# A two-layer graph network on one core: moving the Elu sums and two weight preparations to other places in the queues

## Chip, core and metric

The kernel runs on one core of one Trainium2 chip. The metric is the device time of one execution in microseconds; the time before is the median of three executions, 3022.03 us (3021.59 to 3023.15). The core has five engines with a queue of instructions each: TensorE (PE in the profile, its weight loads PEld), VectorE (DVE), ScalarE (ACT), GpSimd (POOL), and SyncE (SP), which here issues the transfers. Each queue runs in order; across queues, instructions wait for each other by semaphores.

## What is computed

64 graphs of 256 nodes with 512 features share one adjacency matrix `adj`. Two layers follow each other, both with a normalisation in front and a residual around them. The reference, cut to what matters:

```python
# layer 0: masked attention, 8 heads of 64
h = relu(layernorm(x))
q, k, v = h @ Wq + bq, h @ Wk + bk, h @ Wv + bv          # split into heads
scores = q @ k^T / 8 + (1 - adj) * -1e9
x = x + (softmax(scores) @ v) @ Wo + bo
# layer 1: graph attention
h = relu(layernorm(x)) @ W
e = leaky_relu(h @ a1 [rows] + h @ a2 [columns], 0.2) * adj
x = x + elu(softmax(e) @ h + beta * h)
```

All of it is float32.

## The kernel before

Every product with a weight is done in seven block products in place of eight (a 2 x 2 scheme with sums of blocks of the activations and differences of blocks of the weights). So each weight matrix is kept as seven blocks: four are loaded, and `combine` makes four differences of them once at the start, one of which takes the place of a loaded block. Each block product ends in a *tap*, which copies or adds its PSUM bank to its place.

```python
def products(aT, sums, wt, columns, name, taps, across=False):
    plan = (("u", ..., B11), ("v", sums[:, 0], T1), ("u", sums[:, 1], T2), ("c", ..., B21),
            ("u", sums[:, 2], T3), ("v", sums[:, 3], B22), ("u", ..., T4N))
    for (bank, lhs, w_i), tap in zip(plan, taps):      # three banks of ps_mm: u, v, c
        ...                                            # matmuls into the bank
        done = tap(ps)
        if done is not None:
            LAST["tap"] = done                         # the last tap that ran on VectorE and returned itself
        yield                                          # the caller runs so many products at a time
```

For q/k (`project_qk`, line 238) the taps of products 1, 3, 4, 5, 6 and 7 are VectorE additions (lines 311 and 320: q0, k0, q0, k1, k0, q1) and that of product 2 is four ScalarE instructions (line 316). For v and for the second layer's h (lines 330 and 334) products 1, 2, 3 and 7 are copied by ScalarE and 4, 5 and 6 are added by VectorE. For the attention's output `po` all are VectorE additions (line 403). PSUM is shared out in two pools: `ps_big` (2 buffers) and `ps_mm` (4 buffers: q/k, v, output and h products, the transposes `tr_h` and `tr_g`, the two `av`, and a few smaller ones).

The sums and stores of the last step, of graph b:

```python
def gat_sum(b):                      # after the second layer's attention
    ...
    m = p2.tile([P, D], F32, tag="t", ...)      # exp of the row, ScalarE
    o = p2.tile([P, D], F32, tag="o", ...)      # relu of the row, ScalarE
    G[b].append((m, o))

def gat_store(b, t, after=None):     # t: one half of the nodes
    m, o = G[b][t]
    with behind(after):              # queued on its engine after that instruction, no wait for it
        nc.vector.scalar_tensor_tensor(o, m, 1.0, o, op0=ALU.min, op1=ALU.add)                    # L465
        nc.vector.scalar_tensor_tensor(o, o, -1.0, X[b][:, t, :], op0=ALU.add, op1=ALU.add)       # L466
    nc.sync.dma_start(out[b, t * P:(t + 1) * P, :], o)
```

The preparations of the weights Wo and W (Wo with the bias of v worked in):

```python
def prepare_o():
    ps = ps_mm.tile([P, D], F32, tag="mm", name="bvwo")
    nc.vector.tensor_copy(bvb, bv_sb...)                  # bv, each element over a row
    ...                                                   # 16 matmuls: ps = bv @ Wo
    nc.vector.tensor_tensor(bo_sb, bo_sb, ps, ALU.add)    # L186
    nc.scalar.mul(wo_sb[:, :4], wo_sb[:, :4], 1.0 / O_SCALE)
    combine(wo_sb, nc.gpsimd)                             # 4 differences

def prepare_h():
    for j in range(2):
        aj = ...                                          # a1 or a2 on all partitions, by a transfer
        for half in range(2):
            for c in range(2):
                nc.vector.scalar_tensor_tensor(prod, w_sb[...], 1.0 / E_SCALE, aj, ...)     # L199
                nc.vector.tensor_reduce(w_sb[..., FH:FE], prod..., ALU.add)                 # L201
    combine(w_sb, nc.vector)                              # 4 differences
```

And the loop over graphs. TensorE's queue follows the program's order; the order of the other queues is made by the compiler's scheduler from priorities (earlier in the program is higher) and its own timing. One pass works on four graphs at once: b in layer 0, b + 1 in its q/k and v, b - 1 in layer 1, b - 2 in the last sums.

```python
    combine(wqk_sb, nc.vector)
    for b in range(min(2, B)):
        norm(b); norm_apply(b); norm_t(b)
        if b == 0:
            run(project_qk(0), 8)
            prepare_v()
            run(project_v(0), 8)
    prepare_adj()
    for b in range(B + 1):
        ...
        scores(b, (0, 1)); residual(b) if b > 0
        run(project_o(b - 1), 8)
        scores(b, (2, 3), after=LAST.get("pow_y"))
        norm(b + 2)
        qk = project_qk(b + 1)
        run(qk, 1)
        after = LAST["tap"]
        gat_store(b - 2, 0, after)
        gat_norm_apply(b - 1, after)              # shift_y on VectorE, ln_y on ScalarE
        run(qk, 2)
        after = LAST["tap"]
        norm_apply(b + 2, after)                  # shift_x on VectorE, ln_x on ScalarE
        gat_store(b - 2, 1, after)
        load(b + 3)
        run(qk, 2)
        gat_norm_t(b - 1)                         # transposes tr_g, h2T, sums h2sum on VectorE
        run(qk, 3)
        run(gat_h(b - 1), 8)                      # products ph
        values(b)                                 # den, rden, av, oT, osum
        gat_scores(b - 1)
        if b == 0:
            prepare_o(); residual(0); prepare_h()
        norm_t(b + 2)                             # transposes tr_h, hT, hsum
        pv = project_v(b + 1)
        run(pv, 4); gat_sum(b - 1); run(pv, 4)
```

The conditions on b (`if nxt`, `if prev`, `if old`) are left out here. `scores` on GpSimd multiplies each tile of exponentials with the mask (L364) and adds its halves (L366); `residual` adds the bias to x there (L397).

Of the kernel before, what the change touches and what calls it, by code (L numbers as in the profile page):

```python
# [8 lines left out]
F32 = mybir.dt.float32  # L9
AF = mybir.ActivationFunctionType  # L10
ALU = mybir.AluOpType
AX = mybir.AxisListType
PSUM = bass.MemoryType.PSUM

P = 128
# [5 lines left out]
E_SCALE = 2.0 ** -20  # L21
V_SCALE = 2.0 ** -20
D_SCALE = 2.0 ** -60
O_SCALE = 2.0 ** 40
# [4 lines left out]
def tile_gnn_fast(ctx: ExitStack, tc: tile.TileContext, x, adj, wq, bq, wk, bk, wv, bv, wo, bo, w, a, beta, out,  # L29
# [22 lines left out]
    nc = tc.nc  # L52
    B, N, D = x.shape
    H = 8
    HD = D // H
    NT = N // P
    DC = D // P
    NPAIR = H // 2
    HG = H // 4
    HQ = HD // 2  # L60
    FH = D // 2
# [12 lines left out]
    def load(b):  # L74
        X[b] = p2.tile([P, NT, D], F32, tag="x", name=f"x_{b}", bufs=5)
        nc.sync.dma_start(X[b], x[b].rearrange("(t p) c -> p t c", p=P))
# [15 lines left out]
    def combine(wt, eng):  # L92

        for dst, m, n in ((T1, B12, B11), (T3, B22, B12), (T2, B22, T1), (T4N, B21, T2)):
            eng.tensor_tensor(wt[:, dst], wt[:, m], wt[:, n], ALU.subtract)
# [7 lines left out]
    def row(name, src):  # L103
        t = const.tile([P, src.shape[0]], F32, name=name)
        nc.sync.dma_start(t, src.partition_broadcast(P))
        return t
# [10 lines left out]
    for half in range(2):  # L117
        for j in range(2):
            nc.sync.dma_start(wv_sb[:, BLOCKS[half][j]],
                              wv[:, j * FH:(j + 1) * FH].rearrange("(h c p) f -> h p c f", h=2, p=P)[half])  # L120
    if B > 2:
        load(2)


    wo_sb = const.tile([P, 7, 2, FH], F32, name="wo")
# [1 line left out]
    for i in range(4):  # L127
        rows = slice(i * HQ, (i + 1) * HQ)
        for g in range(HG):
            for j in range(2):  # L130
                nc.sync.dma_start(wo_sb[rows, BLOCKS[g][j]],
                                  wo[:, j * FH:(j + 1) * FH].rearrange("(g i d p) f -> i g p d f", g=HG, i=4, d=2)[i, g])
            with nc.allow_non_contiguous_dma(reason="a bias, once"):
                nc.sync.dma_start(bv_sb[rows, g], bv.rearrange("(g i d p) -> i g p d", g=HG, i=4, d=2)[i, g])
    bo_sb = row("bo", bo)

    w_sb = const.tile([P, 7, 2, FE], F32, name="w")
    for half in range(2):
        for j in range(2):
            nc.sync.dma_start(w_sb[:, BLOCKS[half][j], :, :FH],  # L140
                              w[:, j * FH:(j + 1) * FH].rearrange("(h c p) f -> h p c f", h=2, p=P)[half])
    beta_sb = row("beta", beta)

    hs = const.tile([P, NT, 2, FE + 2], F32, name="hs")
    nc.gpsimd.memset(hs[:, :, 1, FE:FE + 1], 1.0)
# [6 lines left out]
    def prepare_adj():  # L152

        some = p3.tile([P, NT], F32, tag="some", name="some", bufs=1)
        empty = p3.tile([P, NT], F32, tag="empty", name="empty", bufs=1)
        full = p2.tile([P, NT, N], F32, tag="g", name="full")
        nc.vector.tensor_reduce(some, adj_sb, AX.X, ALU.add)
        nc.vector.tensor_scalar(empty, some, 0.0, None, ALU.is_equal)
        nc.vector.tensor_scalar(some, some, 0.0, None, ALU.is_gt)
        nc.vector.tensor_reduce(count[:, 1:2], some, AX.X, ALU.add)  # L160
        nc.vector.tensor_tensor(full, adj_sb, adj_sb, ALU.mult)
        nc.vector.tensor_tensor(full, full, adj_sb, ALU.is_equal)
        nc.vector.tensor_reduce(count[:, 0:1], full.rearrange("p t k -> p (t k)"), AX.X, ALU.add)
        for t in range(NT):
            nc.vector.tensor_scalar(full[:, t, :], adj_sb[:, t, :], empty[:, t:t + 1], None, ALU.add)
        ps = ps_mm.tile([P, NT, N], F32, tag="mm", name="adj_t")
        for k in range(NT):
            for t in range(NT):
                nc.tensor.transpose(ps[:, k, t * P:(t + 1) * P], full[:, t, k * P:(k + 1) * P], ident)
        nc.vector.tensor_scalar(adjT, ps, E_SCALE, None, ALU.mult)  # L170
# [4 lines left out]

    def prepare_o():

        ps = ps_mm.tile([P, D], F32, tag="mm", name="bvwo")
        bvb = p2.tile([P, HG, 2, P], F32, tag="t", name="bvb")
        nc.vector.tensor_copy(bvb, bv_sb.unsqueeze(3).to_broadcast([P, HG, 2, P]))  # L180
        for j in range(2):
            for g in range(HG):
                for d in range(2):
                    nc.tensor.matmul(ps[:, j * FH:(j + 1) * FH], bvb[:, g, d, :], wo_sb[:, BLOCKS[g][j], d, :],
                                     start=(g + d == 0), stop=(g + d == 2))
        nc.vector.tensor_tensor(bo_sb, bo_sb, ps, ALU.add)  # L186
        nc.scalar.mul(wo_sb[:, :4], wo_sb[:, :4], 1.0 / O_SCALE)
        combine(wo_sb, nc.gpsimd)

    def prepare_h():  # L190

        for j in range(2):
            aj = p2.tile([P, 2, FH], F32, tag="o", name=f"a_{j}")
            nc.sync.dma_start(aj.rearrange("p i f -> p (i f)"), a[j * D:(j + 1) * D, 0].partition_broadcast(P))
            for half in range(2):
                first, second = BLOCKS[half]
                for c in range(2):
                    prod = p2.tile([P, 2, FH], F32, tag="t", name=f"prod_{j}_{half}_{c}")
                    nc.vector.scalar_tensor_tensor(prod, w_sb[:, first:second + 1:second - first, c, :FH],  # L199
                                                   1.0 / E_SCALE, aj, op0=ALU.mult, op1=ALU.mult)  # L200
                    nc.vector.tensor_reduce(w_sb[:, BLOCKS[half][j], c, FH:FE], prod.rearrange("p i f -> p (i f)"),  # L201
                                            AX.X, ALU.add)
        combine(w_sb, nc.vector)


    def block(aT, t, half):
# [42 lines left out]
    def run(steps, n):  # L249
        for _ in range(n):  # L250
            next(steps, None)

    def behind(ins):

        return tc.issue_after(ins.ins) if ins is not None else nullcontext()
# [83 lines left out]
    def project_v(b):  # L339

        v = V[b] = p2.tile([P, NT, D], F32, tag="v", name=f"v_{b}", bufs=1)
        yield from products(HT[b], HSUM[b], wv_sb, FH, f"pv_{b}",
                            natural_taps(lambda t, j: v[:, t, j * FH:(j + 1) * FH]))
        del HT[b], HSUM[b]
# [117 lines left out]
    def gat_store(b, t, after=None):  # L462
        m, o = G[b][t]
        with behind(after):
# [3 lines that stand above are left out]
        if t == NT - 1:  # L468
            del X[b], G[b]

    with tc.manual_schedule(engines={mybir.EngineType.PE}):
        combine(wqk_sb, nc.vector)
        for b in range(min(2, B)):
            norm(b)
            norm_apply(b)
            norm_t(b)
            if b == 0:
                run(project_qk(0), 8)
                prepare_v()
                run(project_v(0), 8)  # L480
        prepare_adj()

        for b in range(B + 1):
            here, nxt, prev, old = b < B, b + 1 < B, 0 <= b - 1, 0 <= b - 2
            if here:
                scores(b, (0, 1))
                if b > 0:
                    residual(b)
            if prev:
                run(project_o(b - 1), 8)  # L490
            if here:
                scores(b, (2, 3), after=LAST.get("pow_y"))
            if b + 2 < B:
                norm(b + 2)
            qk = project_qk(b + 1) if nxt else iter(())
            run(qk, 1)
            after = LAST["tap"] if nxt else None
            if old:
                gat_store(b - 2, 0, after)
            if prev:  # L500
                gat_norm_apply(b - 1, after)
            run(qk, 2)
            after = LAST["tap"] if nxt else None
            if b + 2 < B:
                norm_apply(b + 2, after)
            if old:
                gat_store(b - 2, 1, after)
            if b + 3 < B:
                load(b + 3)
            run(qk, 2)  # L510
            if prev:
                gat_norm_t(b - 1)
            run(qk, 3)
            if prev:
                run(gat_h(b - 1), 8)
            if here:
                values(b)
            if prev:
                gat_scores(b - 1)
            if b == 0:  # L520
                prepare_o()
                residual(0)
                prepare_h()
            if b + 2 < B:
                norm_t(b + 2)
            pv = project_v(b + 1) if nxt else iter(())
            run(pv, 4)
            if prev:
                gat_sum(b - 1)
            run(pv, 4)  # L530
        for t in range(NT):
            gat_store(B - 1, t)
# [229 lines left out]
```

## Time and profile before

| | before |
|---|---|
| time, median of three | 3022.03 us |
| span of the profiled execution | 3023.4 us |
| granted TensorE clock, mean | 0.993 |
| GpSimd busy | 1867.1 us (62%) |
| ScalarE busy | 1086.8 us (36%) |
| moved from and to memory | 39.85 MB read, 33.55 MB written |

Busy time is the time in which an engine executes, added up; a line of a group gives the busy time, the mean of one instruction and then the idle time of that engine just in front of the group, with what ended it. A line of the waits reads: who waited, for whom, total us, number of times, the longest. A line of the timeline reads: start in us, duration in us, engine, line of the source, operation, output and inputs, shapes, how many were merged; in brackets the idle time in front and what ended it. The span falls into a start of about 125 us, some 61 passes of the loop that are alike, and an end of about 80 us in which no next graph is left.

### The profile page before, as it was taken

The numbers are of one execution on the slowest core, as the hardware profiler recorded it, in microseconds if no ns is written. First come the engines' busy times: TensorE is split into PE (matmuls) and PEld (weight loads), VectorE is DVE, ScalarE is ACT, GpSimd is POOL, SyncE is SP. The second block draws the span as 40 slices with busy tenths as digits, with TensorE's granted clock in tenths as the row PEclk, the third lists the DMA queues.
The fourth block names the chain that finished last, engine by engine and source line by source line (L and its number), as shares of the span: only waits on it lengthen the run. The fifth ranks groups of instructions, "written<-read, shape, count | busy, mean of one in ns | idle before, by whom it ended". The sixth has DMA issues, their size and how long they took to land.

```text
span 3023.4 us, 52940 instructions
## 1 busy us (share of the span) xinstructions
PE 2915.5 (96%) x21910; PEld 2469.9 (82%) x21910; DVE 1907.0 (63%) x3244; ACT 1086.8 (36%) x1987; POOL 1867.1 (62%) x1427
## 2 busy tenths in 40 slices
PE   7999999999999999999999999999999999999996
PEld 6888888888888888888888888888888888888884
DVE  7656656666666566566666665665666666656654
ACT  2333333333333333334333333333343333333332
POOL 6765756656666656566566566575565665666742
PEclk9999999999999999999999999999999999999997
DMA  3000000000000000000000000000000000000000
GB/s 119 15 15 29 22 21 29 18 25 29 15 29 29 15 29 23 21 29 19 25 29 15 29 29 15 29 24 20 29 18 26 29 15 29 29 15 29 22 15 15
DMA packets 43173, 76.86 MB, mean 25 GB/s; under 512 B 5424, under 2 KB 8752, under 8 KB 42928
## 3 DMA queue, kind: packets, MB, share of 16 engines
q1 hardware_dynamic: 42928, 73.42, 7.5%
q8 instruction: 175, 2.87, 0.4%
q14 instruction: 70, 0.57, 0.1%
HBM read 39.85 MB, written 33.55 MB: 24 GB/s over the span
## 4 chain that ended last, share of the span: by engine, by line
PE 86%; DVE 9%; issue 3%; POOL 1%; ACT 0%; DMA 0%; SPq 0%; POOLq 0%; ACTq 0%; DVEq 0%
PE qk_u L238 12%; PE sc L355 8%; PE pg L445 8%; PE po_u L242 8%; PE ph_u L242 7%; PE qk_v L238 7%; PE av L384 7%; PE pv_u L242 7%; DVE o L466 4%; PE ph_v L242 4%; PE po_v L242 4%; PE pv_v L242 4%; PE den L374 2%; PE ph_c L242 2%; PE po_c L242 2%
## 5 line engine op out<-in xcount | busy, mean ns | idle before, releaser
L364 POOL TENSOR_TENSOR s<-s,adjT 128x1024 f32<-128x1024 f32 x256 | 634.6, 2479 | 8.8 <-ACT s L359 7.0
L359 ACT ACTIVATE s<-sc 128x1024 f32<-128x1024 f32 x256 | 248.3, 1021 | 442.2 <-PE sc L355 429.2
L366 POOL TENSOR_TENSOR e<-s 128x512 f32<-128x512 f32 x256 | 351.1, 1371 | 15.3
L427 POOL COPY s1b<-hs 128x256 f32<-128x256 f32 x64 | 25.4, 397 | 522.0 <-ACT hs L330 522.0
L388 POOL TENSOR_TENSOR oT<-oT,rden 128x512 f32<-128x512 f32 x128 | 191.5, 1496 | 241.4 <-PE av L384 222.2
L403 DVE TENSOR_TENSOR x<-po_u,x 128x256 f32<-128x256 f32 x256 | 107.5, 420 | 264.9 <-PE po_u L242 264.9
L377 DVE RECIPROCAL rden<-den 128x512 f32<-128x512 f32 x64 | 214.9, 3357 | 89.4 <-PE den L374 89.4
L238 PE MATMUL qk_u<-hT,wqk 128*128 128x128 f32 x2048 | 258.8, 280 | 2.7 <-DVE kT L320 2.7
L238 PEld LDWEIGHTS qk_u<-hT,wqk 128*128 128x128 f32 x2048 | 241.0, 193 | 24.3 <-issue 20.9
L238 PE MATMUL qk_u<-hsum,wqk 128*128 128x128 f32 x2048 | 251.2, 276 | 5.7 <-DVE kT L311 4.5
L355 PE MATMUL sc<-qT,kT 64*128 64x256 f32 x2048 | 255.8, 389 | 0.3 <-ACT s L359 0.3
L238 PE MATMUL qk_v<-hsum,wqk 128*128 128x128 f32 x2048 | 249.6, 275 | 0.0
L238 PEld LDWEIGHTS qk_u<-hsum,wqk 128*128 128x128 f32 x2048 | 240.2, 193 | 6.3 <-DVE kT L311 4.8
L445 PE MATMUL pg<-hs,eT 128*128 128x256 f32 (+1 forms) x1024 | 238.2, 386 | 7.0 <-ACT eT L436 7.0
L330 ACT COPY hs<-ph_u 128x257 f32<-128x257 f32 x192 | 71.7, 373 | 473.2 <-PE ph_u L242 473.2
L238 PEld LDWEIGHTS qk_v<-hsum,wqk 128*128 128x128 f32 x2048 | 238.9, 192 | 0.0
L355 PEld LDWEIGHTS sc<-qT,kT 64*128 64x128 f32 x2048 | 187.2, 186 | 59.8 <-issue 42.0
L384 PE MATMUL av<-s,v 128*32 128x256 f32 x4096 | 232.7, 379 | 0.0
L445 PEld LDWEIGHTS pg<-hs,eT 128*128 128x128 f32 x1024 | 196.9, 193 | 37.6 <-ACT eT L436 7.8
L216 POOL TENSOR_TENSOR hsum<-hT 128x256 f32<-128x256 f32 x128 | 91.4, 735 | 210.1 <-ACT m L457 197.7
L466 DVE SCALAR_TENSOR_TENSOR o<-o,x 128x512 f32<-128x512 f32 x128 | 212.2, 1658 | 2.1
L384 PEld LDWEIGHTS av<-s,v 128*32 128x32 f32 x4096 | 133.0, 110 | 88.3 <-issue 0.4
(129 smaller groups left out, 5947.9 us busy)
## 6 DMA issues: line engine op xcount, KB each, us to landing
x<-in_x_dram SPq DMA_DIRECT2D x64, 512.0 KB, 3.8
out_dram<-o SPq DMA_DIRECT2D x128, 256.0 KB, 2.1
wqk<-in_L_gnn_Wq_dram SPq DMA_DIRECT2D x2, 512.0 KB, 6.4
wqk<-in_L_gnn_Wk_dram SPq DMA_DIRECT2D x2, 512.0 KB, 7.5
wv<-in_L_gnn_Wv_dram SPq DMA_DIRECT2D x4, 256.0 KB, 5.7
wo<-in_L_gnn_Wo_dram SPq DMA_DIRECT2D x16, 64.0 KB, 2.1
w<-in_L_gnn_W_dram SPq DMA_DIRECT2D x4, 256.0 KB, 5.5
a<-in_L_gnn_a_dram SPq DMA_DIRECT2D x2, 256.0 KB, 6.0
```

The lines of the kernel that those rows point to most:

```text
L238: nc.tensor.matmul(ps[:, d * P:(d + 1) * P], wt[:, w_i, c, d * P:(d + 1) * P], lhs[:, c, :], start=fresh and c + d == 0, stop=(c == 1), sk ...
L242: nc.tensor.matmul(ps, lhs[:, c, :], wt[:, w_i, c, :], start=fresh and c == 0, stop=(c == 1), skip_group_check=True)
L355: nc.tensor.matmul(ps[:, h, t, :], KT[b][hs_, hp, t * P:(t + 1) * P], QT[b][hs_, hp, :], start=True, stop=True)
L359: nc.scalar.activation(s.rearrange("p h k q -> p (h k q)"), ps.rearrange("p h k q -> p (h k q)"), AF.Exp, scale=QSCALE)
L364: nc.gpsimd.tensor_tensor(flat, flat, adjT.rearrange("p k q -> p (k q)").unsqueeze(1) .to_broadcast([P, 2, NT * N]), ALU.mult)
L366: nc.gpsimd.tensor_tensor(e2, s[:, :, 0, :], s[:, :, 1, :], ALU.add)
L377: nc.vector.reciprocal(rden, den)
L384: nc.tensor.matmul(ps[i * HQ:(i + 1) * HQ, d, :], V[b][:, k, c0:c0 + HQ], S[b, 2 * g + i // 2][:, i % 2, k, :], start=(k == 0), stop=(k == ...
L388: nc.gpsimd.tensor_tensor(oT[:, g], oT[:, g], rden[:, g].unsqueeze(1).to_broadcast([P, 2, N]), ALU.mult)
L403: return lambda ps: nc.vector.tensor_tensor(m, ps, m, ALU.add)
L445: nc.tensor.matmul(ps[:, j, :n], eT[:, k, t * P:(t + 1) * P], hs[:, k, j, :n], start=(k == 0), stop=(k == NT - 1))
L466: nc.vector.scalar_tensor_tensor(o, o, -1.0, X[b][:, t, :], op0=ALU.add, op1=ALU.add)
```

## The change

Three things move; hardly any arithmetic changes.

1. Both halves of `gat_store(b - 2)` and the load of graph b + 3 are put behind the seventh product of q/k: the sums are queued on VectorE behind the last tap that reads q/k's banks. Before, one half stood behind the first tap and one behind the third. The aim is that the sums don't stand between TensorE's banks and their readers.
2. `prepare_o` runs right after the first graph's v, before the second graph's transposes, so that its work on ScalarE and GpSimd lies beside the first scores. The scaling of Wo now comes before the product with bv, and the sum scales the product back. In the loads, the bias of v comes after all of Wo, and x of graph 2 after W and beta.
3. `prepare_h` keeps its place in the program, but its VectorE instructions are queued behind the last tap of the second graph's q/k.

```diff
-    if B > 2:
-        load(2)
 ... (loads of Wo: the eight loads of bv move out of their loop, to after it)
     beta_sb = row("beta", beta)
+    if B > 2:
+        load(2)
 ...
     def prepare_o():
+        nc.scalar.mul(wo_sb[:, :4], wo_sb[:, :4], 1.0 / O_SCALE)
         ps = ps_mm.tile([P, D], F32, tag="mm", name="bvwo")
 ...
-        nc.vector.tensor_tensor(bo_sb, bo_sb, ps, ALU.add)
-        nc.scalar.mul(wo_sb[:, :4], wo_sb[:, :4], 1.0 / O_SCALE)
+        nc.vector.scalar_tensor_tensor(bo_sb, ps, O_SCALE, bo_sb, op0=ALU.mult, op1=ALU.add)
         combine(wo_sb, nc.gpsimd)
-    def prepare_h():
+    def prepare_h(after):
+        with behind(after):
 ... (the body as before, indented)
                 run(project_v(0), 8)
+                prepare_o()
 ...
             run(qk, 1)
             after = LAST["tap"] if nxt else None
-            if old:
-                gat_store(b - 2, 0, after)
             if prev:
                 gat_norm_apply(b - 1, after)
             run(qk, 2)
             after = LAST["tap"] if nxt else None
             if b + 2 < B:
                 norm_apply(b + 2, after)
-            if old:
-                gat_store(b - 2, 1, after)
-            if b + 3 < B:
-                load(b + 3)
             run(qk, 2)
             if prev:
                 gat_norm_t(b - 1)
             run(qk, 3)
+            if old:
+                for t in range(NT):
+                    gat_store(b - 2, t, LAST["tap"] if nxt else None)
+            if b + 3 < B:
+                load(b + 3)
 ...
             if b == 0:
-                prepare_o()
                 residual(0)
-                prepare_h()
+                prepare_h(LAST["tap"])
```

## The prediction

> **What bounds the kernel now.** I read the page's first table first: TensorE is busy 96% of the span, VectorE 63%, GpSimd 62%, so TensorE is the engine to fill, and 3023.4 − 2915.5 = 108 us of it are idle. Then I asked the waits (who waited for whom: total us, times, longest) and the groups by line. These lines carry the argument:
>
> ```profile
> PE 2915.5 (96%) x21910; PEld 2469.9 (82%) x21910; DVE 1907.0 (63%) x3244; ACT 1086.8 (36%) x1987; POOL 1867.1 (62%) x1427
> ...
> PE tr_g L283 <- DVE qT L320: 61.2, 61, 1.0
> ...
> L466 DVE SCALAR_TENSOR_TENSOR o<-o,x 128x512 f32<-128x512 f32 x128 | 212.2, 1658 | 2.1
> L465 DVE SCALAR_TENSOR_TENSOR o<-m,o 128x512 f32<-128x512 f32 x128 | 164.1, 1282 | 0.0
> ```
>
> The second line is more than half of TensorE's idle time, and it is one wait: 61 times, once in nearly every graph, 1.0 us each. The two groups below it are the Elu sums. Their means, 1658 and 1282 ns, are far above their shortest forms (678 and 677 ns when I asked for each line by itself), so they are held up by something. The timeline of one graph in the middle shows by what:
>
> ```profile
> 1018.13 0.69 DVE L311 TENSOR_TENSOR kT<-qk_u,bk 128x512 f32<-128x512 f32 x1 [0.29 <-PE qk_u L238]
> 1018.74 0.25 DVE L272 SCALAR_TENSOR_TENSOR shift_x<-mv,rstd_x 128x2 f32<-128x2 f32 x1
> 1018.91 0.68 DVE L465 SCALAR_TENSOR_TENSOR o<-m,o 128x512 f32<-128x512 f32 x1
> 1018.93 2.89 POOL L364 TENSOR_TENSOR s<-s,adjT 128x1024 f32<-128x1024 f32 x1
> ...
> 1019.63 2.74 DVE L466 SCALAR_TENSOR_TENSOR o<-o,x 128x512 f32<-128x512 f32 x1
> 1022.29 0.68 DVE L320 TENSOR_TENSOR qT<-qk_c,qT 128x512 f32<-128x512 f32 x1
> ...
> 1023.12 0.63 PE L283 MATMUL tr_g<-ident,ln_y 128*128 128x128 f32 x4 [1.01 <-DVE qT L320]
> ```
>
> The sum at L466 starts at 1019.63 and ends only when GpSimd's mask multiplication (L364, to 1021.82) has ended. Behind it in VectorE's queue stands the tap that reads q/k's bank `qk_c`, whose matmuls had ended at about 19.9. Four buffers of `ps_mm` are shared by q/k's three banks and the transposes `tr_g`; the second transpose needs the buffer that this tap frees, and TensorE stands for 1.01 us. A graph takes 46.17 us (the same tap at 1022.29 and, one graph on, at 1068.47).
>
> The start has its own waits, about 11 us of idle time between 15 and 96 us besides the first load:
>
> ```profile
> 47.98 2.05 PE L238 MATMUL qk_u<-hsum,wqk 128*128 128x128 f32 x16 [1.68 <-DVE kT L311]
> 54.21 2.90 PE L238 MATMUL qk_u<-hT,wqk 128*128 128x128 f32 x16 [2.40 <-DVE kT L320]
> ...
> 70.02 1.13 PE L242 MATMUL pv_v<-wv,hsum 128*128 128x256 f32 x4 [2.31 <-DVE bo L186]
> 95.74 3.41 PE L238 MATMUL qk_u<-hsum,wqk 128*128 128x128 f32 x16 [2.77 <-DVE kT L311]
> ```
>
> Behind the first three stands the preparation of W on VectorE, between and before the taps; behind the fourth a GpSimd that is late with graph 1, because from 70 to 82 us it did three residuals (2.35 each) and the four differences of Wo (1.26 each).
>
> **What the Trainium skill says.** "SBUF — State Buffer", section "Who interferes with whom": a VectorE instruction with two SBUF inputs and a GpSimd instruction that reads SBUF use one port, held for a whole instruction, and the later one blocks fully. The trace agrees: L466 took 2.74 us beside L364 and 0.68 to 0.69 us where GpSimd was idle (the last graphs), while the taps, with one input in PSUM, keep about 0.68 throughout. "TensorE: Matmul & The Clock Gate", Part 1, says that TensorE falls to half its clock after an idle window. The trace agrees where waits were long: the 16 matmuls after the 2.77 us wait took 3.41 us instead of 2.05; after the steady 1.0 us wait four transposes took 0.63 against 0.60. Removing the steady wait therefore gains the wait and no clock.
>
> **The change part by part.**
>
> *Elu sums behind the last q/k reader.* No instruction is removed or added: four of VectorE per graph (two L465, two L466), two stores and one load move. Between kT's first tap and qc's tap there then remains `shift_x` alone (two SBUF inputs, 2 elements). GpSimd in the same stretch loses its own blocks: L364 took 2.89 against 2.35, the two L366 1.34 and 1.60 against 1.27, together about 0.9 us. I shift its chain: pow_x to 17.2, L366 to 18.5, L364 18.5 to 20.9. In the worst case `shift_x` (asked at 18.74) waits for that L364, to 20.95; the tap of qc then takes 0.68 and ends at 21.6. The second transpose is due after the first, at 21.5 + 0.6 = 22.1. So the 1.0 us wait goes, with about half a microsecond to spare.
>
> Where do the four go? The next taps of VectorE that TensorE needs are those of `ph` (L334). Before, VectorE idles 2.48 us in front of the first of them, then 0.44, 0.44 and 1.41 (before the reciprocal). GpSimd ran its residual L397 at 1023.46 for 2.35 us and then nothing until 1033.88, so the four sums run there unblocked: the last graph but two shows the four in a row from 2939.80 to 2942.74 with a 0.42 tap among them, so about 2.7 us. In the new time (TensorE 1.0 us earlier, L397 ending at about 24.6, the four differences `h2sum` 1.4 us behind it at 26.0, two taps to 27.2) they end at about 29.9. The first `ph` tap is due at 1030.90 − 1.01 = 29.89, and one displaced by up to 0.44 is made up by the gap behind it. The estimate is thus that nothing new waits: 61 × 1.0 = **61 us** gained, the graph 45.17 us. The stores land later, but their buffers are needed only when `gat_sum` writes the next `o` at about 1046, and the x loaded behind them is first read in the next graph's moments (the page: 3.8 us to landing, against 20 and more available).
>
> *Wo beside the first scores.* Sixteen matmuls (3.72 us in one go at 62.25), one copy, one scaling of 1.91 us on ScalarE, and four differences on GpSimd (5.0 us) move from after graph 0's values to before graph 1's transposes. TensorE's work is the same. ScalarE idles from 19.3 to 28.2 and GpSimd from 25.4 to 35.0, so both fit. The sixteen loads of Wo no longer alternate with eight of the bias and come before them: SyncE issued them from 12.26 to about 26, and now Wo should be complete a few us earlier. I allow 1.5 us of new waiting before the matmuls (bias late, or ScalarE busy). GpSimd is relieved of 5.0 us at 72 to 82, so graph 1 should not see the 2.77 us wait; with the clock (3.41 − 2.05) and the longer transposes behind it (1.36 − 1.04) that is 4.5 us.
>
> *W behind the second q/k.* The 8 products, 8 sums and 4 differences on VectorE leave the taps of the second q/k: 1.68 + 2.40 us of waiting, (2.90 − 2.05) + (1.83 − 1.07) of slow clock after it, and 2.31 for the bias sum that stood behind W's differences: 8.0 us. But the block now starts at about 56 and is long: 8 × (0.61 + 0.68) + 4 × 0.7 = 13 us unblocked, plus the reciprocal (3.36), plus blocks by GpSimd's residuals. It stands ahead of the taps of the second v in program order, as before (L287 of graph 2 ran at 69.89, behind all of it, though its transposes ended at 66.9). TensorE needs those taps at about 66 and may get them at 75: I take 6 us back. Sum of the start: −4.5 − 8.0 + 1.5 + 6 = **−5 us**, the least certain term. The end has no q/k and stays.
>
> Total: 3022.0 − 61 − 5 = **2956 us**.
>
> **Rivals.** (a) *The Elu sums become a wait before `ph`'s taps.* The gap of 2.48 is as long as the four sums; the seventh product of `ph` starts 0.17 us after the fifth's tap ended (1032.20 to 1032.37). If they ended 0.5 to 0.8 us later than I think, 0.2 to 0.5 us per graph come back, 12 to 30 us: 2970 to 2985. For it: the tight gap. Against: GpSimd idles in that stretch. (b) *`shift_x` takes the place of L466*, blocked longer than I reckon: half the gain, about 2990. For it: at 95.75 `shift_x` took 1.22 us. Against: it can wait for one GpSimd instruction only. (c) *The start loses.* VectorE's solid block of W delays the second v by 10 us or more: 2965 to 2970 in all. (d) *GpSimd becomes the bound*: no, 62% busy with 8 us of idle time in each graph.
>
> **Range and chances.** The 61 us are the sum of waits on record, and TensorE's order is fixed by hand; only a new wait can take from them. Start −12 to +4; rival (a) or (b) in part at one in six. Range 2945 to 2972. A gain of 2% lies at 2961.6, only 6 us above my value, so faster by over 2% 0.69, within 2% 0.30, slower 0.01.
>
> **What would show it.** Right: the waits lose the line of `tr_g` for qT; L465 and L466 have means near 0.7 us and stand behind the last tap of qT; a graph takes 45.1 to 45.3 us; VectorE's busy time falls by some 200 us with no instruction less, and L364's mean falls. Graph 1's q/k has no 2.8 us wait. Wrong: a wait of TensorE's `ph_u` for the taps L334 or of `tr_g` for anything in every graph, or a wait of over 8 us at the second v near 70 us.

## The result and the profile after

The kernel with all three moves takes **2955.06 us** (median of four executions, 2954.51 to 2956.06), the kernel before 3021.81 us beside it: ratio 0.9779, 95% interval 0.9762 to 0.9796. The time lies 1 us from the forecast; its parts do not lie so well.

First the page's table of engines, and its groups of VectorE and GpSimd that answer to those shown of before. (In the kernel after, line numbers are three higher than before: the Elu sums are L468 and L469, `shift_x` and `shift_y` L275, the mask L367, the taps L314, L323 and L337.)

```profile
PE 2903.1 (98%) x21910; PEld 2468.7 (84%) x21910; DVE 1885.2 (64%) x3244; ACT 1095.5 (37%) x1987; POOL 1787.4 (61%) x1427
```

The groups by line (busy us, mean ns of one, then idle time in front):

```profile
L275 DVE SCALAR_TENSOR_TENSOR shift_x<-mv,rstd_x 128x2 f32<-128x2 f32 x64 | 125.6, 1962 | 0.7 <-POOL rstd_x L268 0.7
L275 DVE SCALAR_TENSOR_TENSOR shift_y<-finite,rstd_y 128x2 f32<-128x2 f32 x64 | 89.2, 1394 | 1.6 <-POOL rstd_y L268 1.6
L469 DVE SCALAR_TENSOR_TENSOR o<-o,x 128x512 f32<-128x512 f32 x128 | 82.5, 684 | 0.0
L468 DVE SCALAR_TENSOR_TENSOR o<-m,o 128x512 f32<-128x512 f32 x128 | 82.3, 682 | 0.0
```

And what `shift_x` was in the kernel before:

```profile
L272 DVE SCALAR_TENSOR_TENSOR shift_x<-mv,rstd_x 128x2 f32<-128x2 f32 x64 | 17.6, 275 | 0.8 <-POOL rstd_x L265 0.7
```

(`shift_x` and `shift_y` are the two small instructions that prepare the normalisations, `rstd_x` and `rstd_y` the powers in front of them on GpSimd.) TensorE's busy share is up to 98%. The Elu sums fell from 164.1 + 212.2 to 82.3 + 82.5 us, to the length that they have with nothing beside them: 212 us less. Yet VectorE's busy time fell by only 22 us, because two instructions of 2 elements each are held now: `shift_x` rose by 108 us, `shift_y` from 14.8 to 89.2. Busy time here is largely time in which an instruction stands and is held.

One graph in the middle of the timeline after, VectorE first, then GpSimd, then TensorE:

```profile
998.49 0.69 DVE L314 TENSOR_TENSOR kT<-qk_u,bk 128x512 f32<-128x512 f32 x1 [1.55 <-PE qk_u L241]
999.10 2.04 DVE L275 SCALAR_TENSOR_TENSOR shift_x<-mv,rstd_x 128x2 f32<-128x2 f32 x1
1001.06 0.68 DVE L323 TENSOR_TENSOR qT<-qk_c,qT 128x512 f32<-128x512 f32 x1
...
1007.07 0.68 DVE L314 TENSOR_TENSOR qT<-qk_u,bq 128x512 f32<-128x512 f32 x1
1007.66 1.28 DVE L468 SCALAR_TENSOR_TENSOR o<-m,o 128x512 f32<-128x512 f32 x2
1008.86 1.29 DVE L469 SCALAR_TENSOR_TENSOR o<-o,x 128x512 f32<-128x512 f32 x2
1010.07 0.42 DVE L337 TENSOR_TENSOR hs<-ph_c,hs 128x257 f32<-128x257 f32 x1
```

```profile
996.88 0.70 POOL L268 TENSOR_TENSOR rstd_x<-rstd_x,mhalf 128x2 f32<-128x2 f32 x1
997.53 1.28 POOL L369 TENSOR_TENSOR e<-s 128x512 f32<-128x512 f32 x1
998.77 2.36 POOL L367 TENSOR_TENSOR s<-s,adjT 128x1024 f32<-128x1024 f32 x1
```

```profile
1001.87 1.04 PE L286 MATMUL tr_g<-ident,ln_y 128*128 128x128 f32 x8
1002.74 1.95 PE L241 MATMUL qk_v<-hsum,wqk 128*128 128x128 f32 x16
```

`shift_x` is now asked while GpSimd's mask runs (998.77 to 1001.13) and ends with it. The tap of `qk_c` stands behind it and ends at 1001.74. That is 0.13 us before TensorE even begins the eight transposes, which run in one go: nothing waits. The four sums run back to back behind the last tap and end at 1010.15, just when the first `ph` tap starts.

`shift_x` has kept its place right behind kT's first tap; what moved is the mask. The sums had held GpSimd as well: of the three instructions above, `rstd_x` took 1.15 us before, the addition of halves 1.34 and the mask 2.89 (at 1016.52, 1017.63 and 1018.93). Now they take 0.70, 1.28 and 2.36, so the mask ends 1.04 us earlier: before, 0.31 us behind the start of the first transpose (1021.82 and 1021.51), now 0.74 us ahead of it (1001.13 and 1001.87). In both kernels the tap of `qk_c` stands behind an instruction that this mask holds. Measured from the first transpose, the tap now comes 1.59 us earlier: 1.04 us because the mask ends sooner, and 0.55 because L466 ran on for 0.55 us behind the mask, where `shift_x` is done at once.

**Where the 70 us are.** I cut both traces at TensorE's first scores of graph 2 (125.11 us before, 128.24 after) and its first scores of graph 63 (2941.01 and 2871.55). Between the cuts lie 61 graphs. The first two numbers of a windows line are the stretch and its length, the third is TensorE's busy time (its instructions in brackets); then the weight loads, VectorE, ScalarE and GpSimd, and at the end the granted clock, the DMA share and GB/s. Before:

```profile
125.11:2941.01 2815.90, 2754.47 (x20855) 2337.87 (x20855) 1786.00 (x3045) 1028.29 (x1888) 1763.72 (x1340) 1.00 0.07 23
```

After:

```profile
128.24:2871.55 2743.31, 2743.04 (x20856) 2339.18 (x20855) 1769.67 (x3045) 1036.56 (x1888) 1684.18 (x1340) 1.00 0.07 24
```

The start lost 3.1 us, the 61 graphs gained 72.6 (1.19 each), and the end gained 0.5 (82.4 to 81.9). Together that is 70.0 us. The medians differ by 66.8, because the profiled execution of before was itself 3.2 us above its median; single executions scatter by some 3 us, and differences of that size between stages are read with this in mind.

Why 1.19 us for a wait that the profile gave as 1.0? Before, TensorE's idle time between the cuts is 2815.90 − 2754.47 = 61.4 us, the 61.2 us of the wait. After, it is 0.3. The rest of the gain, 2754.47 − 2743.04 = 11.4 us, came out of *busy* time, with the same matmuls: 0.187 us per graph. The timeline of before shows where it sat:

```profile
1021.51 0.60 PE L283 MATMUL tr_g<-ident,ln_y 128*128 128x128 f32 x4
...
1023.58 1.95 PE L238 MATMUL qk_v<-hsum,wqk 128*128 128x128 f32 x16
```

Four transposes alone last 0.60 us to the end of the last one, and eight in one go 1.04: the second four add 0.44. So the last 0.16 us of a group normally lie under the next matmul. A wait lays them open, and the profile, which models the ends of matmuls, books them as busy. "TensorE: Matmul & The Clock Gate" of the Trainium skill, Part 2, "Single matmul latency", gives (398 + N)/2.4 ns for a single bf16 matmul at full clock; its constant part, 398/2.4 = 166 ns as an estimate, is of that size. The matmuls here are float32, and no run shows what the 0.16 us are made of. From the first transpose to the next q/k it was 1023.58 − 1021.51 = 2.07 us before and 1002.74 − 1001.87 = 0.87 after, a difference of 1.20.

### The profile page after: what moved, and what is told of

It is laid out like the page before. It is cut to its first block, busy times and chain, and to the rows that moved or that the text cites. A ratio compares the mean times of both kernels' runs of the same rounds, so it can differ in the third digit from the quotient of the medians.

```text
span 2953.4 us, 52881 instructions
## 1 busy us (share of the span) xinstructions
PE 2903.1 (98%) x21910; PEld 2468.7 (84%) x21910; DVE 1885.2 (64%) x3244; ACT 1095.5 (37%) x1987; POOL 1787.4 (61%) x1427
## 4 chain that ended last, share of the span: by engine, by line
PE 97%; DVE 1%; POOL 1%; issue 0%; DMA 0%; ACT 0%; SPq 0%; DVEq 0%; POOLq 0%; ACTq 0%
PE qk_u L241 16%; PE sc L358 8%; PE po_u L245 8%; PE pg L448 8%; PE ph_u L245 8%; PE qk_v L241 8%; PE pv_u L245 7%; PE av L387 7%; PE qk_c L241 4%; PE po_v L245 4%; PE ph_v L245 4%; PE pv_v L245 4%; PE den L377 2%; PE tr_g L286 2%; PE ph_c L245 2%; PE po_c L245 2%
## 5 line engine op out<-in xcount | busy, mean ns | idle before, releaser
L367 POOL TENSOR_TENSOR s<-s,adjT 128x1024 f32<-128x1024 f32 x256 | 603.5, 2357 | 12.6 <-ACT s L362 11.1
L369 POOL TENSOR_TENSOR e<-s 128x512 f32<-128x512 f32 x256 | 326.0, 1273 | 15.3
L460 ACT ACTIVATE m<-g,rsum 128x512 f32<-128x512 f32 x128 | 92.4, 722 | 222.3 <-DVE g L456 222.3
```

What stands on the lines that cost most here:

```text
L367: nc.gpsimd.tensor_tensor(flat, flat, adjT.rearrange("p k q -> p (k q)").unsqueeze(1) .to_broadcast([P, 2, NT * N]), ALU.mult)
L369: nc.gpsimd.tensor_tensor(e2, s[:, :, 0, :], s[:, :, 1, :], ALU.add)
L460: nc.scalar.activation(m, g, AF.Exp, scale=r)
```

## The experiments

All are edits of the kernel before or after, and their times are medians. "Start" is where graph 2's first scores begin in the profiled execution; what lies behind it takes 2822.5 to 2826.0 us in all kernels in which the sums have moved, except the one with the extra instruction. Differences of some 2 us in this column are within what single executions scatter: "sums only" and "only the second half's sums" have the same start and show 125.2 and 123.1.

| kernel | sums | Wo early | W behind q/k | time, us | range | start, us |
|---|---|---|---|---|---|---|
| before | | | | 3021.8 | 3020.6 to 3023.2 | 125.1 |
| after | x | x | x | 2955.1 | 2954.5 to 2956.1 | 128.2 |
| sums only | x | | | 2950.7 | 2949.0 to 2952.3 | 125.2 |
| only the second half's sums | half | | | 2950.8 | 2948.7 to 2953.3 | 123.1 |
| start only | | x | x | 3025.8 | 3023.6 to 3029.6 | 128.9 |
| after, extra minimum | x | x | x | 2994.4 | 2992.8 to 2995.5 | 128.6 |
| after, residual later | x | x | x | 2951.0 | 2949.8 to 2951.8 | 124.5 |
| after, W behind the second v | x | x | later | 2957.3 | 2956.3 to 2958.8 | 130.8 |
| both of these | x | x | later | 2948.2 | 2946.9 to 2952.2 | 124.1 |
| sums and W | x | | x | 2957.7 | 2954.7 to 2957.9 | 130.0 |
| sums and Wo | x | x | | 2951.1 | 2950.7 to 2953.3 | 127.2 |
| sums and Wo, residual later | x | x | | 2947.5 | 2946.1 to 2948.7 | 123.2 |
| both, and W's differences on GpSimd | x | x | later | 2943.5 | 2942.9 to 2946.6 | 118.8 |

The kernel before, run beside the later ones, took 3022.7 to 3023.3 us. The profile of "sums and Wo" is of its slowest execution (2953.3), so its start is rather too late than too early.

### The sums alone

The kernel before, with part 1 alone:

```diff
+            if old:                        # behind the seventh product
+                for t in range(NT):
+                    gat_store(b - 2, t, LAST["tap"] if nxt else None)
+            if b + 3 < B:
+                load(b + 3)
```

> The kernel before with the Elu sums, stores and the load alone moved behind q/k's last reader; Wo and W prepared where they were. Theory A (the whole gain is the one wait per graph, and it costs the shift from one start to the next, 46.17 - 44.97 = 1.20 us, not the 1.01 us of idle time that the profile gives it; the start loses about 3 us): 3021.8 - 61 x 1.20 = 2949 us, faster than the full change by 6. Theory B (as the prediction had it: 1.0 us per graph from the sums, the rest from the start): 2960 us, slower than the full change by 5.

Measured: 2950.73 us, ratio 0.9762 (0.9745 to 0.9778). All the start's waits of before stand where they stood, and the wait of `tr_g` for qT is gone. So the sums bring 72 us, more than the whole change brings, and parts 2 and 3 together cost some 4 us.

### Only the second half's sums

```diff
             if old:
                 gat_store(b - 2, 0, after)     # first half stays behind the first tap
 ...
-                for t in range(NT):
+                for t in range(1, NT):         # second half behind the seventh product
```

> The kernel before with only the second half of the nodes' sums (those that stood behind the third tap) moved behind the last one; the first half's two sums stay behind the first tap. Theory A (the wait comes from one instruction, the sum that GpSimd's mask multiplication blocks ahead of the tap of bank c): the wait goes as a whole, 2949 to 2952 us. Theory C (each half costs its share, because any work of VectorE between the taps delays them): half of the gain, about 2985 us.

Measured: 2950.78 us, ratio 0.9765 (0.9748 to 0.9781), the same as with both halves moved. The wait was thus made by the second half's pair, in the trace by the one L466 that the mask held. VectorE's timeline with the first half left in place:

```profile
1037.32 0.69 DVE L466 SCALAR_TENSOR_TENSOR o<-o,x 128x512 f32<-128x512 f32 x1
...
1040.10 0.69 DVE L320 TENSOR_TENSOR qT<-qk_c,qT 128x512 f32<-128x512 f32 x1 [0.93 <-PE qk_c L238]
```

The tap of `qk_c` now waits 0.93 us for its matmuls. The reader is ahead of TensorE instead of behind it. And nothing between the taps is held: the mask starts at 1039.11, behind `shift_x` at 1038.92, which keeps its length of before.

```profile
L272 DVE SCALAR_TENSOR_TENSOR shift_x<-mv,rstd_x 128x2 f32<-128x2 f32 x64 | 17.5, 273 | 0.8 <-POOL rstd_x L265 0.7
```

So the hold on `shift_x` in the kernel after comes from moving the first half too: GpSimd is then so far ahead that its mask starts before `shift_x` is asked. It costs nothing, and moving the first half brings nothing. The load of graph b + 3 moved along with the sums in all these kernels; no wait for it shows in the traces, but it was not moved by itself.

### The start alone

The kernel after, with the sums put back between the taps (parts 2 and 3 alone).

> The changed kernel with the sums, stores and the load put back between the taps: only the preparations of Wo and W and the order of the loads are changed. Theory A: the start costs 3 us (graph 2's first scores begin at 128.2 instead of 125.1 us) and the per-graph wait stays: 3025 us. Theory B: the start gains 5 us: 3017 us.

Measured: 3025.84 us, ratio 1.0009 (1.0003 to 1.0016), 3 us slower than before. The waits of this kernel still have the line that the sums' move takes away:

```profile
PE tr_g L286 <- DVE qT L323: 61.2, 61, 1.0
```

The two halves of the change add up within the scatter: −72 and +3 make −69, against −67 in the medians. Parts 2 and 3 together lose time by themselves.

### How much room is left before the `ph` taps

One more VectorE minimum in each half, on top of the kernel after; it changes no value, since the minimum with 1 is taken anyway:

```diff
     with behind(after):
+        nc.vector.scalar_tensor_tensor(m, m, 1.0, m, op0=ALU.min, op1=ALU.min)
```

> The changed kernel with one more VectorE instruction of the same size in front of each half's sums (a minimum of m with itself and 1, which leaves the result as it is): 2 x 0.6 us more per graph behind the last tap. If the room there is as tight as rival (a) has it (the seventh product of ph starts 0.17 us after the fifth's tap has ended): the tap comes about 0.8 us late, the product waits 0.6 us in each graph, 2955 + 61 x 0.6 = 2992 us. If all the gaps up to the reciprocal count as room (2.5 + 0.44 + 0.44 + 1.4 us against 3.8 us of work): no change, 2955 us.

Measured: 2994.41 us, 39 us above the kernel after, 39.35/61 = 0.645 us per graph. Two instructions of 0.68 us, 1.28 in a row, bring 0.645: about half of them found room. The waits and TensorE's timeline:

```profile
PE ph_u L245 <- DVE hs L337: 22.4, 60, 0.4
```

```profile
1024.62 1.14 PE L245 MATMUL ph_u<-w,h2T 128*128 128x257 f32 x4 [0.37 <-DVE hs L337]
```

VectorE's timeline shows the sums end at 1023.90 and three `ph` taps follow without a gap:

```profile
1022.62 1.28 DVE L470 SCALAR_TENSOR_TENSOR o<-o,x 128x512 f32<-128x512 f32 x2
1023.82 0.42 DVE L337 TENSOR_TENSOR hs<-ph_c,hs 128x257 f32<-128x257 f32 x1
1024.15 0.41 DVE L337 TENSOR_TENSOR hs<-ph_u,hs 128x257 f32<-128x257 f32 x1
```

So the forecast's rival (a) is real and begins some 0.6 us later than the sums now end. The idle time again understates it: 0.37 us against 0.645. The starts give the whole. From the sixth product to the seventh it is 1.40 us here (1023.22 to 1024.62) and 0.87 in the kernel after; from the seventh to `den` 1.07 and 0.96; 0.53 + 0.11 = 0.64. The first of these is again 0.16 us above the idle time.

### Which part of the start loses: the residuals

In the trace after, TensorE has two waits at graph 0's `den` (the matmuls that sum the masked exponentials) that the kernel before has not, and the `av` (the products with v) behind them run slowly (6.58 us, against 3.63 before). TensorE:

```profile
56.85 0.62 PE L377 MATMUL den<-e,dsum 128*32 128x256 f32 x4 [1.11 <-POOL e L369]
...
60.94 0.64 PE L377 MATMUL den<-e,dsum 128*32 128x256 f32 x2 [3.46 <-POOL e L369]
61.38 6.58 PE L387 MATMUL av<-s,v 128*32 128x256 f32 x62
...
80.59 2.07 PE L245 MATMUL pv_u<-wv,hT 128*128 128x256 f32 x4 [6.42 <-DVE v L337]
```

GpSimd in front of them:

```profile
37.73 2.37 POOL L400 TENSOR_TENSOR x<-x,bo 128x1024 f32<-128x1024 f32 x1 [0.19 <-DVE bo L189]
...
42.09 2.37 POOL L400 TENSOR_TENSOR x<-x,bo 128x1024 f32<-128x1024 f32 x1
...
45.75 2.38 POOL L367 TENSOR_TENSOR s<-s,adjT 128x1024 f32<-128x1024 f32 x1
```

Since Wo's preparation is early, `bo` is ready early, and two residuals run on GpSimd ahead of the first mask, which starts at 45.75 instead of 38.37; with the following edit it starts at 42.30. The edit to the kernel after queues the residuals of graphs 0 to 2 behind the last mask sum:

```diff
-                nc.gpsimd.tensor_tensor(e2, s[:, :, 0, :], s[:, :, 1, :], ALU.add)
+                LAST["halves"] = nc.gpsimd.tensor_tensor(e2, s[:, :, 0, :], s[:, :, 1, :], ALU.add)
 ...
-        nc.gpsimd.tensor_tensor(X[b], X[b], bo...)
+        with behind(LAST["halves"] if b < 3 else None):
+            nc.gpsimd.tensor_tensor(X[b], X[b], bo...)
```

> The changed kernel with the first three residuals on GpSimd queued behind the latest mask multiplications traced so far, so that they no longer run ahead of graph 0's. If the 1.1 and 3.5 us waits of den and the half clock behind them (av 6.58 instead of 3.64 us) come from the residuals that the early Wo let in: 7.5 us less, 2947.5 us, and the wait of the second v for VectorE stays at about 6 us. If VectorE's block of W alone sets when the second v ends: the time that den gains is waited out there, and 2953 to 2955 us remain.

Measured: 2950.98 us, ratio 0.9764 (0.9747 to 0.978), 4.1 us under the kernel after. The `den` waits fell to 0.62 us in all and `av` to 3.83. But the wait at the second v grew from 6.42 to 9.15:

```profile
76.49 2.07 PE L245 MATMUL pv_u<-wv,hT 128*128 128x256 f32 x4 [9.15 <-DVE v L337]
```

So the residuals were a cause, but the kernel gains 4.1 us only, though TensorE's waits at `den` are 3.95 us shorter and its `av` another 2.75. VectorE's queue shows why. The reciprocal of `den` (`rden`) stands ahead of nearly all of W's block, and W's block ahead of the taps of v. In the kernel after:

```profile
62.05 3.36 DVE L380 RECIPROCAL rden<-den 128x512 f32<-128x512 f32 x1 [4.71 <-PE den L377]
...
78.98 0.41 DVE L337 TENSOR_TENSOR v<-pv_c,v 128x256 f32<-128x256 f32 x1
```

With the edit:

```profile
57.72 3.36 DVE L380 RECIPROCAL rden<-den 128x512 f32<-128x512 f32 x1 [0.18 <-PE den L377]
...
74.89 0.41 DVE L337 TENSOR_TENSOR v<-pv_c,v 128x256 f32<-128x256 f32 x1
```

The whole chain comes 4.3 us earlier at the reciprocal and 4.1 at the tap, and 4.1 us is what the kernel gains. TensorE's slow `av` matmuls run beside this chain and cost nothing here: in "start only" they took 5.67 us in place of 6.58, the wait at the second v was 7.85 in place of 6.42, and `pv_u` went on at 80.73, no earlier than the 80.59 above.

### W's block: further back

The kernel after, with `prepare_h` behind all products of the second v in the program, still queued behind the last q/k tap:

```diff
-                prepare_h(LAST["tap"])
+                last_qk = LAST["tap"]
 ...
             run(pv, 4)
+            if b == 0:
+                prepare_h(last_qk)
```

> The changed kernel with W's preparation put after the second v in the program, still behind the last tap of the second q/k: the taps of v then have the higher priority in VectorE's queue. If the 6.4 us wait of the second v comes from the place of W's block in the queue: that wait goes, with the slow clock behind it (2.07 - 1.03 and 2.67 - 2.00): 8 us less, 2947 us. If VectorE simply has too much to do there: under 3 us less, and the wait moves to po.

Measured: 2957.34 us, ratio 0.9787 (0.9771 to 0.9803), 2 us above the kernel after. The wait at v is down to 0.74, but a new one stands at the output's product:

```profile
86.78 2.05 PE L245 MATMUL po_u<-wo,osum 128*128 128x256 f32 x4 [7.90 <-DVE x L406]
```

W's block is moved behind v's taps and now stands in front of `po`'s. With the residual edit as well:

> Both repairs of the start on the changed kernel. If the two losses are separate: 2955.1 - 7.5 - 8.1 = 2939.5 us, 11 under the sums alone. If they are one delay seen twice: 2947 us.

Measured: 2948.2 us, ratio 0.9758 (0.9742 to 0.9774). The residual's gain is kept this time and more than that (9 us under the kernel with W moved alone), yet `po` still waits 7.9 us. VectorE's timeline in front of it:

```profile
74.73 1.75 DVE L95 TENSOR_TENSOR w<-w 128x514 f32<-128x514 f32 x1
...
77.11 3.79 DVE L95 TENSOR_TENSOR w<-w 128x514 f32<-128x514 f32 x2
80.83 0.41 DVE L407 TENSOR_TENSOR x<-po_u,x 128x256 f32<-128x256 f32 x1
```

What is left in the way are mostly W's differences: each has two SBUF inputs, about 0.68 us long alone, and up to 3.79 for two when held by GpSimd. Three of them, 5.5 us, stand ahead of `po`'s first tap.

### W's move without Wo's, and Wo's without W's

First the sums and part 3, with `prepare_o` where it was before:

> The sums moved, and W's VectorE work behind the second q/k, with Wo prepared where it was. Against the sums alone (2950.7 us): the waits in the second q/k (1.7 + 2.4 us and 1.5 us of slow clock) and that for the bias sum (2.3 us) go, 8 us; W's block stands before the taps of the second v, 6 to 9 us; graph 1's wait (2.8 us and 1.2 of slow clock) stays. Sum: 2949 to 2952 us. If the loss of the start were Wo's alone: 2943 us. If it were W's alone: 2955 us.

Measured: 2957.67 us, ratio 0.9784 (0.9768 to 0.98), 7 us above the sums alone and above all three forecasts. The second v waits longest of all here:

```profile
81.21 2.07 PE L243 MATMUL pv_u<-wv,hT 128*128 128x256 f32 x4 [12.29 <-DVE v L335]
```

Then the sums and part 2, the kernel after with W's VectorE work free to run as early as the scheduler puts it:

```diff
-        with behind(after):
+        with behind(None):
```

> The changed kernel without the queueing of W's VectorE work behind the second q/k (parts one and two of the change alone). In the scheduler's order most of W's work then stands before and between the taps of the second q/k, some 10 us earlier. If part three is what costs the start: the 6.4 us wait of the second v and 1.7 us of slow clock go, some 2 to 4 us of waits in the second q/k come back: 2949 to 2952 us. If part three is what it pays for: over 2957 us.

Measured: 2951.07 us, ratio 0.9762 (0.9745 to 0.9778), 4 us under the kernel after and level with the sums alone. The wait at v is gone, but the second q/k waits 6.71 us (`qT`) and 3.03 us (`kT`), more than the 1.68 and 2.40 of the kernel before: six of W's eight products now run between 40.8 and 52.2 us, two at a time, ahead of the first tap. So part 2 has gained the waits for `bo` (2.31 us) and at graph 1's q/k (2.77), and lost as much here. With the residual edit on top:

> The same with the first residuals queued behind the mask multiplications, the repair that gave 4 us on the full change. If W's late block had swallowed half of that gain (den's waits and slow clock were 7.5 us): here all of it shows, 7 us under the run without it, 2943 to 2945 us. If not: 4 us under it.

Measured: 2947.49 us, ratio 0.9749 (0.9732 to 0.9765), 3.6 us less, much the same as the 4.1 that this edit brought in the kernel after. But it came another way, and so decides nothing between the two forecasts: without part 3 TensorE reaches `den` only at 69.65 us and doesn't wait there. Between the two profiles the start is 4.04 us shorter, and only 0.76 of it are shorter waits in the second q/k. About 3.5 us are slow matmuls behind the waits, and no run shows why the clock stayed up in one of the two. Without the edit:

```profile
65.94 3.79 PE L241 MATMUL qk_u<-hT,wqk 128*128 128x128 f32 x16 [3.03 <-DVE kT L323]
```

With the edit:

```profile
64.67 2.05 PE L241 MATMUL qk_u<-hT,wqk 128*128 128x128 f32 x16 [2.59 <-DVE kT L323]
```

### W's differences on GpSimd

The four differences of W are taken off VectorE in the version with both edits:

```diff
-            combine(w_sb, nc.vector)
+            combine(w_sb, nc.gpsimd)
```

> Both repairs, and W's four differences on GpSimd instead of VectorE. Where both repairs stood, VectorE had 8.0 us of them before po's second and third tap while TensorE waited 7.9 us, and GpSimd is idle for 7 us behind. If the load of VectorE before po is the limit: 4 to 6 us under both repairs, 2943 us. If GpSimd blocks VectorE's products as much by its own work: no gain, 2948 us.

Measured: **2943.52 us**, ratio 0.974 (0.9724 to 0.9756): under both kernels, and 4.7 us under the same version with the differences on VectorE. `po` now waits 1.45 us in place of 7.9:

```profile
75.39 1.10 PE L245 MATMUL po_u<-wo,osum 128*128 128x256 f32 x4 [1.45 <-DVE x L407]
...
118.84 2.00 PE L358 MATMUL sc<-qT,kT 64*128 64x256 f32 x16
```

Graph 2 starts at 118.84, 6.3 us earlier than before the change and 9.4 earlier than after it. GpSimd pays some of it back: a new wait of 1.58 us stands at graph 1's q/k.

## Why the total held, and which steps did not

**"61 × 1.0 = 61 us gained, the graph 45.17 us."** The mechanism is right: the line of `tr_g` for qT is gone, the sums have means of 682 and 684 ns and stand behind the last tap of qT, and with one half's sums alone moved the whole gain is there. The size is not. A graph takes 44.97 us (the same tap at 994.92 and 1039.89), below the 45.1 to 45.3 that I named, and 61 graphs gained 72.6 us. The step that failed is the reading of a wait's worth: I took the idle time, which begins only at the modelled end of the matmul before it, and left out the 0.19 us of a broken stream. The forecast said that "removing the steady wait therefore gains the wait and no clock"; it is right on the clock (1.00 in both stretches), and wrong on the wait.

**`shift_x` "to 20.95; the tap of qc then takes 0.68 and ends at 21.6 … half a microsecond to spare".** This is what happened, nearly to the tenth: `shift_x` is held for 2.04 us, to the end of the mask, and the 64 of them have a mean of 1962 ns. The reckoning behind it, GpSimd's chain earlier by about 0.9 us once the sums are out of its way, was right too: 1.04 us. Of rival (b), the cause occurred and the cost did not. The port rule ("SBUF — State Buffer", "Who interferes with whom") names no least size of an instruction; the trace shows 2 elements held to the end of the mask, as 512 were.

**"They end at about 29.9", with the first `ph` tap due at 29.89.** The sums end as the first tap starts (1010.15 and 1010.07), and TensorE doesn't wait. The room was larger than the equal numbers suggested. The extra minimum measured it: about 0.6 of its 1.28 us were free.

**"VectorE's busy time falls by some 200 us."** It fell by 22. The sums did lose 212 us, but I put the blocked time down as the sums' own. The masks now hold `shift_x` and `shift_y` instead. L367's mean fell from 2479 to 2357 ns and GpSimd's busy time by 80 us, as forecast in kind.

**"Sum of the start: −4.5 − 8.0 + 1.5 + 6 = −5 us."** It lost 3 us in the profile, and the start alone 3.0 in the medians: the term is wrong in sign. Term by term:
- The −4.5 came: graph 1's q/k has no wait. The waits of the second q/k and of `bo` went too.
- The +1.5 for Wo failed. The matmuls of `bvwo` waited only 0.58 us. But "both fit" counted what the preparation adds to GpSimd, not what it sets free: with `bo` early, residuals ran ahead of the first masks. The new waits at `den` are 1.11 + 3.46 us, and with them the reciprocal and all of VectorE's work behind it comes later. With the residuals queued behind the masks, the kernel takes 4 us less.
- The +6 for the block of W at the second v was about right in this kernel (6.42 of waiting, and 7.85 and 8.2 in the two others with the same start), but only because TensorE came late: with the residuals out of the way it waits 9.15, and without part 2 12.29. The forecast named over 8 us there as a sign of being wrong; the kernel after is under it, three of the variants (8.2, 9.15 and 12.29) go over it.

The experiments tell these two apart: added to the sums alone, part 3 costs about 7 us, and about 4 where part 2 is there too; part 2 without part 3 is level with leaving Wo where it was; with the residuals queued later it lies 3.2 us under it. The terms don't add, as the same stretch of VectorE's queue sets TensorE's delay in both.

So 2956 was met to 1 us by luck: the Elu term was some 11 us too small and the start's term 8 us too good. What stays open: why the scheduler put the residuals before the masks and W's products before the q/k taps; how far the slow scores behind `pv_u` are a cost of their own; and what the order of the loads and the scaling, which came with Wo's earlier place, do by themselves.

## What to carry to other kernels

Size a steady wait of TensorE by the distance from start to start of the matmuls around it, with and without the wait, and not by the idle time: here 1.2 us against 1.0, and 0.64 against 0.37. When a preparation moves earlier, list what its result sets free and where that runs; and a block of work that is moved off one set of taps stands in front of the next, unless a part of it goes to another engine (here worth 4.7 us). Ask in both directions who holds whom: the sums were held by GpSimd and had also made it late. Run each part of a change alone: here half of part 1 gained all, and parts 2 and 3 paid only once they were mended.

## What the runs showed of the hardware that I had not expected

- A VectorE instruction on 128 x 2 elements with two SBUF inputs lasted 2.04 us beside a GpSimd mask that had begun 0.33 us before it, against 0.25 us where the mask began 0.19 us after it: its mean went from 275 to 1962 ns though its place behind kT's tap stayed, because the mask came earlier.
- A break in TensorE's stream cost about 0.19 us over the idle time that the profile counts (11.4 us over 61 breaks).
- Waits of 1.11 and 3.46 us, 4.1 us apart, were followed by `av` matmuls of 6.58 us in place of 3.63; the clock granted between 61 and 64 us was 0.50, and 1.00 again from 68 us. 61 waits of 1.0 us, one in 46 us, left it at 1.00. "TensorE: Matmul & The Clock Gate", Part 1, describes such a fall after an idle window of some 3.4 us. The trace agrees with the fall, but not with 3.4 us as the least idle time: the clock fell to 0.50 behind waits of 2.40 and 2.77 us before the change too (at 56 and 97 us), while behind the 2.59 us in "sums and Wo, residual later" it stayed at 1.00. That the two waits close together made the fall at 61 us is argued from their place only.
